# A group-normalised 3x3 convolution: statistics for 12 images at a time, measured further ahead

## The chip, the cores and the metric

The kernel runs on one core of a Trainium2 chip. The metric is the device time of one execution in microseconds (us), lower being better. The kernel before has a median of 968.84 us over three runs (968.79 to 969.57). The engines are named as in the profile: PE is TensorE (matrix products), PEld its weight loads, DVE is VectorE, ACT is ScalarE, POOL is GpSimd, and SP is SyncE, which here only issues DMAs.

## The reference

The input is 160 images of 128 channels and 32x32 pixels (float32). Each is normalised over groups of four channels, a 3x3 convolution with quantised weights is applied, and the image itself is added back:

```
def _gn(v, G=32, eps=1e-5):
    ...
    m = jnp.mean(g, axis=(2, 3, 4), keepdims=True)
    s = jnp.var(g, axis=(2, 3, 4), keepdims=True)
    return ((g - m) / jnp.sqrt(s + eps)).reshape(v.shape)
...
xb = x.reshape(B // N, N * C, H, W)
act = jax.lax.conv_general_dilated(xb, w, window_strides=(STRIDE, STRIDE), padding=[(PAD, PAD), (PAD, PAD)], dimension_numbers=('NCHW', 'OIHW', 'NCHW'), feature_group_count=N)
...
x = x + _L0_conv_ref(_gn(x), L0_conv_U)
```

There are five weight sets; image b*5 + n is convolved with set n. The weights are U rounded down in two steps that depend on the largest and smallest value of U. Here it matters only that every set costs some vector and scalar work, done while the images of the set before are convolved.

## The kernel before, in words

**Order of the images.** One loop (`for i in range(self.imgs)`, L1106) runs over 160 images, 32 of each weight set in turn. Each engine executes its instructions in the order in which this loop emits them. There are no planned times: what an engine waits for is decided by data and by buffers.

**An image in the pipeline.** Iteration i works on several images at once:

- ScalarE measures one image some way ahead, in two passes over its 1024 pixels. The first sums them (L241, stage 0), the second sums the squares of the differences (L248, stage 1). In the loop, stage 0 stands at the head of ScalarE's part of the iteration, ahead of `residual(i-1)`; stage 1 stands at its tail. Eight images, `BY_VECTOR = (8, 10, 11, 14, 19, 24, 29, 34)`, are measured by VectorE instead.
- For image i+4, POOL and VectorE take the mean off and combine neighbouring columns into a tile v of 2048 values ("combined" images: POOL L675 and L705 in `beside_pairs`, VectorE L687 and L694 in `combine`), or POOL normalises it into z (L711, the other images). POOL's part is tied to the last but one of VectorE's instructions ahead of `pairs`, so that it runs while VectorE is in `pairs`.
- For image i+3, ScalarE makes the float16 high part (L735 from v, or L645 from z). If the image is the first of its statistics group and not combined, ScalarE also makes z itself first (`normalise`, L637), from the group's `shift` and `rstd`.
- For image i+2, VectorE makes the float16 low part (L741, or L748 and the three operations L761 to L770).
- For image i+1, PE forms the products of rows (`sums_of_pairs`, into the PSUM tiles m1a or m1b, and m2, which is "m" in the profile). ScalarE copies m2 out (`leave`, L888), and VectorE writes both into the image's PSUM bank (`pairs`, L900 and L902).
- For image i, PE adds the rest of the products (`main`), and in the next iteration ScalarE copies the bank to SBUF (`residual`, L926). POOL issues a DMA that adds it to the output (L950). The image itself was stored to the output earlier by SP (`store_input`, L965).

The tile m2 is a single PSUM bank, so `leave` for image i+1 has to be done before PE starts the row products of image i+2.

**Statistics by group.** `cuts` (L472) divides the images into groups: small ones first, then 8 images each from image 24 on, 24 groups in all. `self.groups` and `group_of` follow from it. When the last image of a group has been measured, the group's numbers are made in the three iterations after:

- first: `means` (PE, L256), then on VectorE `deviations_by_vector` (five operations on 128x8 numbers, L296 to L302),
- second: `variances` (PE, L273), and `deviation` on ScalarE (L279),
- third: `power` on POOL (L286, which stands on POOL ahead of `beside_pairs` of image i+4), and after VectorE's `pairs` the two operations of `scales_by_vector` (L307: rstd times a constant; L309: shift = mean times rstd).

How far ahead is measured is set by one line, in which the lead grows by one for every fourth image up to a cap:

```
ahead = i + min(10 + i // 4, self.STAT_LEAD + 1)
to_measure = range(measured, min(self.imgs, ahead))
```

With STAT_LEAD = 14 the cap is reached at iteration 20. In the iterations 8, 12, 16 and 20 there are two images to measure in place of one.

**Loads and stores.** Images come in pairs ("chunks", 1 MB) into 12 buffers. Chunk c + 12 is loaded into the buffer of chunk c; `consumed(c)` says after which iteration that load is emitted, and the DMA itself waits until the buffer's last reader is done. Four iterations after its load is emitted, the chunk is stored to the output. Loads and stores go out on SP's queue, one after the other; the store of a chunk waits there until its load has landed.

Of the kernel before, what the change touches and what calls it, by code (L numbers as in the profile page):

```python
# [8 lines left out]
F32 = mybir.dt.float32  # L9
I32 = mybir.dt.int32  # L10
MM = mybir.dt.float16
ALU = mybir.AluOpType
# [9 lines left out]
NB = 2  # L22
# [14 lines left out]
class Later:  # L37


    def __init__(self, steps=(), pace=0.0):  # L40
        self.steps = iter(steps)
        self.pace, self.due = pace, 0.0
        self.scalar = False
# [19 lines left out]
    def finish(self):  # L63
        run(self.steps)
# [125 lines left out]
def group_mean_matrix(nc, pool):  # L190

    P = nc.NUM_PARTITIONS
    gavg = pool.tile([P, P // GROUP, GROUP], F32, tag="gavg", name="gavg")
    nc.gpsimd.memset(gavg, 1.0 / GROUP)
    nc.gpsimd.affine_select(
        out=gavg, in_=gavg, compare_op=ALU.is_ge, fill=0.0, base=0,
        pattern=[[-GROUP, P // GROUP], [0, GROUP]], channel_multiplier=1,
    )
    nc.gpsimd.affine_select(
        out=gavg, in_=gavg, compare_op=ALU.is_ge, fill=0.0, base=GROUP - 1,  # L200
        pattern=[[GROUP, P // GROUP], [0, GROUP]], channel_multiplier=-1,
    )
    return gavg.rearrange("p g k -> p (g k)")


class Statistics:
# [5 lines left out]
    def __init__(self, nc, small, gavg, mhalf, nb, scale, name):  # L212
        self.nc, self.small, self.gavg, self.mhalf = nc, small, gavg, mhalf
        self.nb, self.scale, self.name = nb, scale, name
        self.late = False

        self.mv = self.tile("mv", [nb, 2])

# [85 lines left out]
    def scales_by_vector(self):  # L304

        vector = self.nc.vector
        vector.tensor_scalar_mul(self.rstd, self.rstd, self.scale)  # L307
        self.shift = self.tile("shift", [self.nb])
        vector.tensor_tensor(self.shift, self.ngm, self.rstd, ALU.mult)  # L309

    def scales(self):
        nc = self.nc
# [8 lines left out]
def general_path(tc, keep, steps, x, u, out):  # L321
# [8 lines left out]
    with tc.If(far > 0), ExitStack() as ctx:  # L330
# [9 lines left out]
        for n in range(N_SETS):  # L340
            un = one.tile([P, C, TAPS], F32, tag="u", name=f"g_u{n}")
            nc.sync.dma_start(un, uv[n])
            wn = one.tile([P, C, TAPS], F32, tag="w", name=f"g_w{n}")
            k1, k2 = run(steps.quantise(one, un, f"g{n}", F32))
            nc.vector.tensor_scalar_mul(wn, k1, steps.s1)
            nc.vector.scalar_tensor_tensor(wn, k2, steps.s2, wn, ALU.mult, ALU.add)
# [38 lines left out]
class Main:  # L385
# [21 lines left out]

    STAT_LEAD = 14  # L410
    LOAD_LEAD = 18
    CHUNKS = 12
    STEADY = 7
# [3 lines left out]
    EARLY = 8  # L417
    FIRST = 3
    HURRIED = (0, 2, 4, 8, 24)


    COLS = (1, 0, 2)
# [3 lines left out]
    def __init__(self, tc, ctx, keep, x, u, out):  # L426
        self.tc = tc
        nc = self.nc = tc.nc
        self.imgs, C, self.H, self.W = x.shape
        P = self.P = nc.NUM_PARTITIONS  # L430
        assert C == P and self.H * self.W == 1024
        self.per_set = self.imgs // N_SETS
        self.xv = x.rearrange("(b n) c h w -> n c b (h w)", n=N_SETS)
        self.ov = out.rearrange("(b n) c h w -> n c b (h w)", n=N_SETS)
        self.uv = u.rearrange("n (o i k) -> n o i k", o=C, k=TAPS)

        def pool(name, bufs, **kw):
            return ctx.enter_context(tc.tile_pool(name=name, bufs=bufs, **kw))

        self.const = pool("const", 1)  # L440
        self.qpool = pool("quant", 1)
        self.wpool = pool("weights", 2)
        self.upool = pool("u", 1)
        self.xpool = pool("x", self.CHUNKS)
        self.zpool = pool("z", 2)
        self.parts = pool("parts", 4)
        self.rows = pool("rows", 4)
        self.wide = pool("wide", 2)
        self.wide_parts = pool("wide_parts", 3)
        self.evac = pool("evac", 2)  # L450
        self.sums = pool("sums", 3)
        self.unread = pool("unread", 1)
        self.small = pool("small", 3)
        self.ps_eo = pool("ps_eo", 2, space=PSUM)
        ps_m = pool("ps_m", 1, space=PSUM)
        ps_small = pool("ps_small", 1, space=PSUM)
        self.steps = Steps(nc, keep)

        self.m1a, self.m1b, self.m2_ps = (
            ps_m.tile([P, self.H // 2, self.W], F32, tag=name, name=name)  # L460
            for name in ("m1a", "m1b", "m2")
        )
        self.pair = [self.m1a, self.m2_ps]

        small = ps_small.tile([P, 512], F32, tag="small", name="small")
        self.pt, self.pg = small[:, : ROW * P].rearrange("p (k o) -> p k o", k=ROW), small[:, ROW * P :]
        self.chunks, self.z, self.hi, self.v, self.eo, self.m2 = {}, {}, {}, {}, {}, {}
        self.sum, self.stored = {}, {}
        self.tables, self.wts, self.across = {}, {}, {}
        self.columns = []  # L470

        cuts = [0, 2, 4, 8, 12, 16, 20, *range(24, self.imgs + 1, 8)]  # L472
        self.groups = [range(a, b) for a, b in zip(cuts, cuts[1:])]
        self.group_of = {i: k for k, g in enumerate(self.groups) for i in g}
        self.stats = {}
# [117 lines left out]
    def keep_sums(self, n, col):  # L593
        wt = self.wts[n, col]
        run(self.both_sums(
            self.nc.gpsimd, wt[:, self.SUM], wt[:, self.DIFF], *(wt[:, k] for k in range(ROW))
        ))
# [9 lines left out]
    def stats_of(self, k):  # L607
        if k not in self.stats:
            self.stats[k] = Statistics(
                self.nc, self.small, self.gavg, self.mhalf, len(self.groups[k]),  # L610
                self.steps.lift, k,
            )
            self.stats[k].late = self.groups[k].start not in self.HURRIED
        return self.stats[k]

    def measure(self, i, stages=(0, 1)):
# [39 lines left out]

    def by_scalar_too(self, i):

        return i < self.FIRST + 4 or i == self.groups[self.group_of[i]].start

    def column_of(self, i):

# [306 lines left out]

    def consumed(self, c):  # L970

        return max(i + 2 if self.by_hand(i) else i - 2 for i in range(c * NB, c * NB + NB))

    def run(self):
        nc, P = self.nc, self.P
# [26 lines left out]
        self.ident5 = self.const.tile([P, P], MM, tag="ident5", name="ident5")  # L1002
        nc.gpsimd.tensor_scalar_mul(self.ident5, ident, 5.0)
        self.gavg = group_mean_matrix(nc, self.const)
        self.mhalf = self.const.tile([P, 8], F32, tag="mhalf", name="mhalf")
        nc.gpsimd.memset(self.mhalf, -0.5)

        self.los = []
# [97 lines left out]
        for i in range(self.imgs):  # L1106
# [30 lines left out]
            else:  # L1137
                j = i - 1
                self.conv(i, on_the_way)
            ahead = i + min(10 + i // 4, self.STAT_LEAD + 1)  # L1140
            to_measure = range(measured, min(self.imgs, ahead))
# [163 lines left out]
```

## Time and profile before

| | before |
|---|---|
| median of three runs | 968.84 us |
| the profiled execution | 968.17 us |
| its span (first to last instruction) | 966.4 us |
| PE busy | 926.9 us (96%) |
| VectorE busy | 910.1 us (94%) |
| ScalarE busy | 862.0 us (89%) |
| POOL busy | 463.6 us (48%) |
| HBM traffic over the span | 262 GB/s |

The profile is of one execution. "Busy" is the time in which an engine had at least one instruction under way. PE's matrix products overlap: one of 512 columns is shown with 0.38 us, but the next starts about 0.21 us later. Idle time in front of an instruction is shown with what ended it ("<-"). The shares are averages over a start of some 50 us, a long middle part, and an end in which no image is left to measure.

### The profile page before, as it was taken

Reading aid. Unit: us, or ns where it says so; the run is one execution under the profiler, and the core shown is the slowest. Engines: PE = TensorE matmul, PEld = TensorE weight load, DVE = VectorE, ACT = ScalarE, POOL = GpSimd, SP = SyncE. Lnnn points to the kernel's source line nnn. Section 1 sums busy time; section 2 is a strip of 40 time slices with the busy share of each in tenths; the row PEclk is TensorE's granted clock in tenths of the full one; section 3 lists DMA queues with packets and bytes.
Section 4 is the critical chain, followed back from the end, with each engine's and each line's share of the span. In section 5 each row is a group of like instructions: output and inputs, shape, how many; then the busy total and the mean of one; then the engine's idle time right before and its main releaser. Section 6 shows DMA issues by size and latency. Waiting matters only on the chain.

```text
span 966.4 us, 13055 instructions
## 1 busy us (share of the span) xinstructions
PE 926.9 (96%) x4432; PEld 433.6 (45%) x4432; DVE 910.1 (94%) x1280; ACT 862.0 (89%) x1167; POOL 463.6 (48%) x477
## 2 busy tenths in 40 slices
PE   2999999999999999999999999999999999999997
PEld 1444444444444444444444444444444444444443
DVE  7999999999999999989999999999999998998995
ACT  5879999999999999999989999999989999998561
POOL 4345344446445444554355435534445545666550
PEclk9999999999999999999999999999999999999999
DMA  9079999999999999999999999999999999666663
GB/s 363 20 273 340 338 328 321 334 322 315 327 320 328 314 327 323 311 315 258 283 243 287 276 305 286 278 251 301 278 274 260 286 275 255 98 90 107 91 107 112
DMA packets 67450, 254.22 MB, mean 263 GB/s; under 512 B 5296, under 2 KB 5296, under 8 KB 67376
## 3 DMA queue, kind: packets, MB, share of 16 engines
q1 hardware_dynamic: 45344, 173.09, 47.6%
q0 software_dynamic: 22032, 80.23, 44.7%
q8 instruction: 36, 0.59, 0.2%
q14 instruction: 38, 0.31, 0.1%
HBM read 89.19 MB, written 164.10 MB: 262 GB/s over the span
## 4 chain that ended last, share of the span: by engine, by line


## 5 line engine op out<-in xcount | busy, mean ns | idle before, releaser
L785 PE MATMUL eo<-hi,wt 128*128 128x496 f16 (+3 forms) x1170 | 310.3, 375 | 0.9 <-ACT wt L567 0.9
L840 PEld LDWEIGHTS <-wt 128*128 128x128 f16 x1884 | 183.9, 99 | 211.5 <-DVE rows L770 1.7
L741 DVE SCALAR_TENSOR_TENSOR vl<-v,rstd,vh 128x2048 f16<-128x2048 f32 x94 | 221.5, 2356 | 1.0 <-ACT vh L735 0.9
L840 PE MATMUL eo<-vh,wt 128*128 128x512 f16 x561 | 210.2, 375 | 0.2 <-DVE eo L902 0.2
L840 PE MATMUL eo<-vl,wt 128*128 128x512 f16 x561 | 210.1, 375 | 0.0
L735 ACT ACTIVATE vh<-v,rstd 128x2048 f16<-128x2048 f32 x94 | 188.1, 2001 | 13.4 <-DVE v L694 13.0
L926 ACT COPY sum<-eo 128x1024 f32<-128x1024 f32 x153 | 160.7, 1050 | 29.4 <-PE eo L840 28.5
L675 POOL TENSOR_SCALAR v<-xt,ngm 128x64 f32<-128x64 f32 x94 | 83.0, 883 | 215.5 <-issue 66.8
L785 PEld LDWEIGHTS <-wt 128*128 128x128 f16 x1242 | 120.9, 99 | 140.2 <-DVE eo L902 2.6
L248 ACT ACTIVATE junk<-xt,mv 128x1024 uint8<-128x1024 f32 x152 | 174.4, 1147 | 0.1
L840 PEld LDWEIGHTS <-across 128*128 128x128 f16 x1128 | 110.3, 98 | 140.3 <-issue 13.3
L241 ACT ACTIVATE junk<-xt 128x1024 uint8<-128x1024 f32 x152 | 160.5, 1056 | 13.8 <-DMA xt<-in_x_dram 10.7
L711 POOL TENSOR_SCALAR z<-xt,ngm,rstd 128x1024 f32<-128x1024 f32 x49 | 90.5, 1847 | 155.9 <-DVE rows L769 45.9
L840 PE MATMUL eo<-rows,wt 128*128 128x512 f16 x378 | 143.5, 380 | 0.0
L950 POOL DMA_DIRECT2D out_dram<-sum x153 | 133.8, 876 | 9.5 <-ACT sum L926 6.1
L840 PE MATMUL m<-vl,across 128*128 128x496 f16 (+1 forms) x282 | 105.6, 374 | 9.5 <-DVE vl L741 9.5
L687 DVE TENSOR_TENSOR v<-xt 128x960 f32<-128x960 f32 x94 | 109.0, 1160 | 0.0
L840 PE MATMUL m<-vh,across 128*128 128x496 f16 (+1 forms) x282 | 105.6, 375 | 0.9 <-ACT m L888 0.9
L888 ACT ACTIVATE m<-m 128x512 f32<-128x512 f32 x157 | 93.8, 597 | 13.4 <-PE m L840 13.2
L705 POOL TENSOR_TENSOR v<-xt 128x512 f32<-128x512 f32 x94 | 97.2, 1034 | 0.0
L748 DVE TENSOR_TENSOR lo<-z,hi 128x1024 f16<-128x1024 f32 x66 | 80.6, 1220 | 0.0
L286 POOL TENSOR_TENSOR rstd<-ve,mhalf 128x8 f32<-128x8 f32 (+2 forms) x24 | 39.1, 1629 | 68.8 <-DVE rows L769 22.0
(150 smaller groups left out, 1182.3 us busy)
## 6 DMA issues: line engine op xcount, KB each, us to landing
xt<-in_x_dram SPq DMA_DIRECT2D x78, 1024.0 KB, 12.7
out_dram<-sum POOLq DMA_DIRECT2D x153, 512.0 KB, 8.8
out_dram<-xt SPq DMA_DIRECT2D x76, 1024.0 KB, 18.6
out_dram<-xt SPq DMA_DIRECT2D x7, 512.0 KB, 3.7
u<-in_L_conv_U_dram SPq DMA_DIRECT2D x4, 576.0 KB, 19.0
xt<-in_x_dram SPq DMA_DIRECT2D x4, 512.0 KB, 9.7
range<-in_L_conv_U_dram SPq DMA_DIRECT2D x3, 576.0 KB, 7.9
u<-in_L_conv_U_dram SPq DMA_DIRECT2D x2, 288.0 KB, 3.2
```

Of the source, the lines that this page charges most:

```text
L241: self.nc.scalar.activation(junk, image, ACTF.Copy, scale=-1.0 / image.shape[1], accum_out=self.mv[:, j, 0:1],)
L248: self.nc.scalar.activation(junk, image, ACTF.Square, bias=self.mv[:, j, 0:1], accum_out=self.mv[:, j, 1:2],)
L687: nc.vector.tensor_tensor(self.view(v, 1, (511, 2), (half, H), (1, half - 1)), self.view(x, 1, (1, 2), (W, H), (2, half - 1)), self.view(x ...
L705: ins = nc.gpsimd.tensor_sub(self.v[i][:, 1536:], odd, even)
L711: ins = nc.gpsimd.tensor_scalar(z, self.image(i), st.ngm[:, j], st.rstd[:, j], ALU.add, ALU.mult)
L735: self.nc.scalar.mul(vh, self.v[i], st.rstd[:, j])
L741: yield self.nc.vector.scalar_tensor_tensor(vl, self.v[i], st.rstd[:, j], self.hi[i], ALU.mult, ALU.subtract)
L785: nc.tensor.matmul(self.bank(target, a)[:, first:end, c0:c1], self.wts[n, col][:, k, :], tile[:, s0 : s0 + 2 * (end - first) - 1 : 2, c0 + ...
L840: self.nc.tensor.matmul(out, weights, moving, start=start and j == 0, stop=False, skip_group_check=True)
L888: self.nc.scalar.mul(m2, self.m2_ps, 0.5)
L926: nc.scalar.copy(self.as_banks(i, self.sum[i]), self.flat(i, eo))
L950: added = self.nc.gpsimd.dma_start(self.ov[n, :, b], self.sum.pop(i), accum_op=ALU.add)
```

## The change

The statistics groups have 8 images up to image 48, then 12 each up to image 144, then 8 again; there are 20 groups in place of 24. The cap of the lead is 20 images in place of 15 (STAT_LEAD 19), so it goes on growing until iteration 40: iterations 24, 28, 32, 36 and 40 now also measure two images. Groups that start at image 32 or later have no `shift` (L309 is left out), and their first image, where it isn't combined, gets its z from POOL like any other and not from ScalarE. The load of chunk c + 12 is emitted one iteration earlier. The constant -0.5 that `power` uses is 16 wide in place of 8.

```
-        self.late = False
+        self.late = self.shifted = False
...
         vector.tensor_scalar_mul(self.rstd, self.rstd, self.scale)
-        self.shift = self.tile("shift", [self.nb])
-        vector.tensor_tensor(self.shift, self.ngm, self.rstd, ALU.mult)
+        if self.shifted:
+            self.shift = self.tile("shift", [self.nb])
+            vector.tensor_tensor(self.shift, self.ngm, self.rstd, ALU.mult)
...
-    STAT_LEAD = 14
+    STAT_LEAD = 19
...
+    BY_SCALAR = 32
...
-        cuts = [0, 2, 4, 8, 12, 16, 20, *range(24, self.imgs + 1, 8)]
+        cuts = [0, 2, 4, 8, 12, 16, 20, 24, 32, 40, *range(48, self.imgs - 12, 12), 152, self.imgs]
...
             self.stats[k].late = self.groups[k].start not in self.HURRIED
+            self.stats[k].shifted = self.groups[k].start < self.BY_SCALAR
...
     def by_scalar_too(self, i):
-        return i < self.FIRST + 4 or i == self.groups[self.group_of[i]].start
+        start = self.groups[self.group_of[i]].start
+        return i < self.FIRST + 4 or i == start and start < self.BY_SCALAR
...
     def consumed(self, c):
-        return max(i + 2 if self.by_hand(i) else i - 2 for i in range(c * NB, c * NB + NB))
+        return max(i + 2 if self.by_hand(i) else i - 3 for i in range(c * NB, c * NB + NB))
...
-        self.mhalf = self.const.tile([P, 8], F32, tag="mhalf", name="mhalf")
+        self.mhalf = self.const.tile([P, 16], F32, tag="mhalf", name="mhalf")
```

## The prediction

> **What bounds the kernel now.** I read the page first, then stretches of the span, then the waits of PE and of ScalarE, and last the timelines where those waits end. The page says PE is busy nearly all the time; the stretches (busy us of each engine, number of instructions in brackets) say more:
>
> ```profile
> core 0: us, PE busy (x) PEld busy (x) DVE busy (x) ACT busy (x) POOL busy (x), PEclk, DMA share, GB/s
> 190.00:291.00 101.00, 101.00 (x485) 47.26 (x483) 97.79 (x136) 96.89 (x132) 49.48 (x49) 1.00 1.04 322
> 291.00:400.00 109.00, 109.00 (x530) 51.51 (x528) 105.62 (x150) 106.42 (x149) 50.26 (x51) 1.00 1.04 321
> 400.00:600.00 200.00, 197.20 (x945) 92.12 (x944) 191.11 (x263) 190.53 (x259) 96.99 (x93) 1.00 1.02 284
> 600.00:800.00 200.00, 198.06 (x951) 92.41 (x950) 193.71 (x266) 190.49 (x260) 96.13 (x95) 1.00 1.00 274
> 800.00:945.00 145.00, 142.10 (x677) 66.18 (x675) 132.75 (x154) 118.04 (x141) 83.51 (x73) 1.00 0.69 122
> ```
>
> The first stretch holds iterations 24 to 40. PE is busy in all of it, so time lost there is lost for good; VectorE and ScalarE are idle for 3.2 and 4.1 us of 101. Three engines stand near their limit at once, and the DMA engines show a share of 1. Only in the last stretch does ScalarE have room. What PE waits for after the start (us in total, times, longest):
>
> ```profile
> PE m L840 <- DVE vl L741: 9.5, 9, 1.9
> PE m L840 <- ACT m L888: 0.9, 1, 0.9
> PE m L840 <- DVE rows L770: 0.8, 1, 0.8
> ```
>
> So about 11 us are lost to engines that come late, nearly all to VectorE's low part. The timeline shows what makes it late (VectorE, then POOL, then PE; start, duration, idle time before):
>
> ```profile
> 810.25 0.70 DVE L902 SCALAR_TENSOR_TENSOR eo<-m1b,m 128x512 f32<-128x512 f32 x1
> 811.17 0.37 DVE L307 TENSOR_SCALAR rstd<-rstd,lift 128x8 f32<-128x8 f32 x1 [0.22 <-POOL rstd L286]
> 811.58 0.96 DVE L309 TENSOR_TENSOR shift<-ngm,rstd 128x8 f32<-128x8 f32 x1
> 812.46 1.15 DVE L687 TENSOR_TENSOR v<-xt 128x960 f32<-128x960 f32 x1
> ...
> 809.43 1.71 POOL L286 TENSOR_TENSOR rstd<-ve,mhalf 128x8 f32<-128x8 f32 x1 [5.91 <-DVE rows L769]
> 811.14 0.37 POOL L675 TENSOR_SCALAR v<-xt,ngm 128x64 f32<-128x64 f32 x1
> 811.48 1.03 POOL L705 TENSOR_TENSOR v<-xt 128x512 f32<-128x512 f32 x1
> ...
> 816.59 0.38 PE L840 MATMUL m<-vl,across 128*128 128x512 f16 x1 [0.97 <-DVE vl L741]
> ```
>
> This is a group's third step. `power` pushes POOL's two operations 1.7 us back; L309, on 8 numbers, lasts 0.96 us until POOL's L705 ends, and L687 starts only then, 1.5 us after `pairs` ends at 810.95. PE pays 0.97 us.
>
> ScalarE's own cost of one measured image, in iteration 25:
>
> ```profile
> 198.43 1.16 ACT L248 ACTIVATE junk<-xt,mv 128x1024 uint8<-128x1024 f32 x1
> 199.49 0.20 ACT L248 ACTIVATION_READ_ACCUMULATOR junk<-xt,mv 128x1 f32 x1
> 199.71 1.06 ACT L241 ACTIVATE junk<-xt 128x1024 uint8<-128x1024 f32 x1
> 200.68 0.19 ACT L241 ACTIVATION_READ_ACCUMULATOR junk<-xt 128x1 f32 x1
> 200.77 1.08 ACT L926 COPY sum<-eo 128x1024 f32<-128x1024 f32 x1
> ```
>
> From 198.43 to 200.77 is 2.34 us, with nothing between.
>
> **What the Trainium skill says.** "SBUF — State Buffer", section "SBUF: two separate sides": VectorE and GpSimd share a port pair under an exclusive lock; a VectorE operation with two SBUF inputs and a GpSimd operation that reads SBUF exclude each other, and whoever starts first holds it to the end. The trace agrees: L309 takes 0.16 us alone and 0.96 us beside L705. So leaving L309 out does not make L687 earlier, since L687 has two SBUF inputs too. "Perfetto Trace Analysis", section "Identifying the Most-Contended Engine": occupancy is a fair measure for Vector and Scalar, a poor one for Tensor. So I looked at the starts: products shown with 0.375 us start every 0.21 us in the PE lines of the timeline, whose overlap could hide a gap of up to 0.16 us; between 190 and 291 us the largest spacing of two starts is 0.23, so nothing is hidden. Section "Optimizing Scalar/DVE Operations" of the same page: each operation has a fixed overhead. The five operations on 128x8 numbers take 0.15 to 0.17 us each, so at 128x12 I take them as unchanged.
>
> **The change part by part**, against the profiled execution's 968.17 us (span 966.4 and 1.77 around it).
>
> *The growing lead.* Images 39, 44, 49, 54 and 59 become second images of iterations 24, 28, 32, 36 and 40. The earlier second images (19, 24, 29, 34) are VectorE's by the list BY_VECTOR, which the change leaves alone; the new ones fall to ScalarE. That is 5 x 2.34 = 11.7 us more in a stretch where ScalarE is idle for 101 - 96.89 = 4.1 us (2.7 waiting for PE at L926, 0.8 at L888). Queued behind the second stage 0 are `residual` and `leave`, and behind the second stage 1 those of the next iteration; `pairs` and PE's next row products wait for them. How late may they be? In the timeline the m copy ends at least about 1.2 us before PE overwrites that bank, in the tightest of five images (226.12 against 227.3 for image 31), and VectorE's start of `pairs` lies 0 to 2.9 us after it. So a backlog of some 1.2 us can be carried over at the end. PE loses 11.7 - 4.1 - 1.3 = **+6.3 us**. Bounds: 4.5 if two images' worth of lag can be carried, 9 if ScalarE's gaps can't be filled because VectorE falls behind with it. The five images that ScalarE is spared at the end (iterations 141 to 145) are worth 0: PE there waits for VectorE only.
>
> *Fewer groups.* From image 48 on there are 10 groups in place of 14. On PE each costs two insertions: products start at 805.14 and 805.50 around one pair of L273, so 0.36 - 0.22 = 0.14 us, twice per group, 4 groups: **-1.1 us**. VectorE saves 4 x 5 x 0.16 = 3.2 us, which counts only through PE's waits, next.
>
> *Third steps.* Of the 9.5 us, 7.65 us precede images 64, 74, 79, 119, 135, 143 and 151, a few images behind such a step. `power` takes 788 ns on 128x2 and 1763 on 128x8, so 0.16 us per number; on 128x12 an estimated 2.4 us. POOL's L675 and L705 and VectorE's L307 and L687 move back by another 0.65 us. From image 32 on there were 16 third steps, 11 beside a combined image; after there are 12, 10 beside a combined one (image p+4 for p = 28, 31, 43, 55, 91, 103, 115, 127, 135, 143). In two (p = 67, 79) POOL also has z, 1.2 to 3.2 us. Fewer steps, each longer. Taking each step's extra lateness against the time the low part had to spare at the next combined image (0.1 us at 59, 0.6 at 49, 1.7 at 94, nothing at 119), I get some 8.2 us lost in place of 7.6: **+0.6 us**. Bounds -7.65 (none is left) and +4.
>
> *No `shift`.* 0.16 us of VectorE where it ran alone, nothing beside L705: 0 on the path, being covered by that lock. Without the cover it would give back up to 0.96 us per step, which is inside the bounds above.
>
> *z by POOL.* ScalarE loses five L637 (images 48, 56, 88, 96, 128), 1.15 us each after overlap: 5.8 us. In their stretch (291 to 400) PE never waits, so 0; it only clears the carried backlog sooner. POOL gains five L711 of about 1.5 us, within its idle half: 0, up to +1.
>
> *Loads.* By order on SP's queue, the loads of chunks 16 to 23 go ahead of one more store each, and from chunk 24 on the order is the same. A store behind them lands some 5 us later, and the POOL DMA that adds image 12 may wait for it for 3 us of POOL's idle time: 0, bounds -1 and +2. Measuring up to five images earlier takes some 29 us off the time between landing and first use. The tightest is the load of images 54 and 55 (SP's queue; the store waits until it has landed):
>
> ```profile
> 226.92 5.42 SPq L495 DMA_DIRECT2D xt<-in_x_dram  x1
> ...
> 257.83 0.38 SPq L965 DMA_DIRECT2D out_dram<-xt  x1
> ```
>
> It lands at 257.8; the changed kernel wants it in iteration 36, which without any delay would begin at 256. Three second images have put ScalarE some 4 us back by then, so 0, bounds 0 and +5. The wider constant is set once, before the loop: 0.
>
> **Sum:** +6.3 - 1.1 + 0.6 = +5.8, so 974.0 us for a profiled execution; the median of runs lies 0.7 above the profiled one, hence **974.6 us**.
>
> **The rivals.** *The backlog is absorbed:* ScalarE's extra passes are taken up by waits and buffers, at 0 to 2 us. The total is 967.8 to 970.3, say 969, no measurable change. Against it: 4.1 us of idle time can't hold 11.7.
>
> *Loads come late:* ScalarE, in order, stands before images 50 to 63 until they land, DMA share being 1.04 there. Every late microsecond adds; some 4 us more give 978.6. For it: the landing margins above vanish. Against it: the delay of the first theory makes room.
>
> *Faster, by the third steps:* placed at other images of the five-image pattern, they no longer meet a low part without time to spare, and the 7.65 us go. With ScalarE's loss between its low end and its middle (4.5 to 6.3) this gives 968.84 - 1.1 - 7.65 + 5.4 = 965.5. It decides once ScalarE's loss is under 6.8 us with all those waits gone, or under 3 with half gone. For it: the same step costs 1.9 us at images 79 and 119 and nothing at others. Against it: each is 0.65 us longer.
>
> **How the numbers follow.** Runs here tell a difference of about 0.2% from none (966.9 to 970.8). Chances: forecast 0.52 (its own range 971 to 978), absorbed 0.10, loads late 0.17, faster 0.21. So faster 0.21, same 0.09, slower 0.70. The range that leaves out about 2 in 10 is 965.5 to 980.
>
> **What would show it.** Right: between 190 and some 300 us ScalarE has no idle time, PE shows gaps before L840 that end with ACT m or DVE vl, and 6 us are lost by iteration 41; `power` on 128x12 at 2.4 us; 8 products fewer each of L256 and L273. Wrong: PE still full from 190 to 300, or ScalarE's gaps ended by DMA, or the waits on vl down to 3 us.

## The result, and the profile after

The changed kernel is slower by 0.21%: 970.9 us against 968.67 us (medians of 20 runs each), a ratio of 1.0021 with a 95% interval of 1.0015 to 1.0028. The forecast was slower by 5.8 us; the loss is 2.2 us. The profiled execution took 971.39 us, its span is 969.6 us.

Three of the same stretches as before the change, of the changed kernel (busy us of PE, PEld, VectorE, ScalarE and POOL in this order):

```profile
190.00:291.00 101.00, 97.28 (x461) 44.55 (x459) 91.85 (x125) 100.27 (x143) 47.66 (x46) 1.00 1.04 328
291.00:400.00 109.00, 106.74 (x510) 49.37 (x509) 105.54 (x142) 103.76 (x143) 50.90 (x50) 1.00 1.03 300
...
800.00:945.00 145.00, 145.00 (x691) 67.59 (x690) 132.44 (x150) 111.96 (x128) 86.20 (x75) 1.00 0.72 131
```

Two things happened at once. In the first stretch, where PE had been full, ScalarE is now busy for 100.27 of 101 us and PE for 97.28; 24 fewer products start in it. In the last stretch PE had 2.9 us without work, and now has none. What PE waits for after the start:

```profile
PE m L844 <- DVE vl L745: 6.4, 8, 1.4
PE m L844 <- ACT m L892: 3.7, 5, 1.0
PE m L844 <- DVE rows L774: 1.6, 3, 0.8
PE eo L844 <- DVE eo L906: 1.2, 4, 0.4
```

Waits on VectorE's low part vl fell from 9.5 to 6.4 us, and waits on ScalarE's copy of m rose from 0.9 to 3.7. The place of the latter is iteration 24, the first with a new second image (timeline of ScalarE, then of PE):

```profile
190.53 1.06 ACT L241 ACTIVATE junk<-xt 128x1024 uint8<-128x1024 f32 x1
191.71 1.06 ACT L241 ACTIVATE junk<-xt 128x1024 uint8<-128x1024 f32 x1
...
196.11 1.15 ACT L248 ACTIVATE junk<-xt,mv 128x1024 uint8<-128x1024 f32 x1
...
197.38 1.15 ACT L248 ACTIVATE junk<-xt,mv 128x1024 uint8<-128x1024 f32 x1
...
200.61 0.60 ACT L892 ACTIVATE m<-m 128x512 f32<-128x512 f32 x1
...
201.26 0.38 PE L844 MATMUL m<-vh,across 128*128 128x512 f16 x1 [1.01 <-ACT m L892]
```

Both passes stand twice in a row, the copy of m ends at 201.21, and PE starts 0.05 us later after 1.01 us without work.

### The profile page after: what moved, and what is told of

Same layout as the page of the kernel before. It is cut to its first block, busy times and chain, and to the rows that moved or that the text cites. A ratio compares the mean times of both kernels' runs of the same rounds, so it can differ in the third digit from the quotient of the medians.

```text
span 969.6 us, 12968 instructions
## 1 busy us (share of the span) xinstructions
PE 928.7 (96%) x4416; PEld 431.4 (44%) x4416; DVE 903.9 (93%) x1240; ACT 857.0 (88%) x1158; POOL 468.7 (48%) x478
## 4 chain that ended last, share of the span: by engine, by line
## 5 line engine op out<-in xcount | busy, mean ns | idle before, releaser
L745 DVE SCALAR_TENSOR_TENSOR vl<-v,rstd,vh 128x2048 f16<-128x2048 f32 x94 | 220.4, 2344 | 0.8 <-ACT vh L739 0.6
L679 POOL TENSOR_SCALAR v<-xt,ngm 128x64 f32<-128x64 f32 x94 | 78.6, 836 | 236.2 <-issue 92.5
L715 POOL TENSOR_SCALAR z<-xt,ngm,rstd 128x1024 f32<-128x1024 f32 x54 | 96.2, 1782 | 161.1 <-DVE rows L773 46.9
L691 DVE TENSOR_TENSOR v<-xt 128x960 f32<-128x960 f32 x94 | 113.3, 1205 | 0.0
L709 POOL TENSOR_TENSOR v<-xt 128x512 f32<-128x512 f32 x94 | 96.9, 1031 | 0.0
L904 DVE SCALAR_TENSOR_TENSOR eo<-m1a,m 128x512 f32<-128x512 f32 x78 | 54.2, 695 | 22.5 <-PE m1a L844 11.6
## 6 DMA issues: line engine op xcount, KB each, us to landing
xt<-in_x_dram SPq DMA_DIRECT2D x78, 1024.0 KB, 10.6
```

Of the source, the lines that this page charges most:

```text
L691: nc.vector.tensor_tensor(self.view(v, 1, (511, 2), (half, H), (1, half - 1)), self.view(x, 1, (1, 2), (W, H), (2, half - 1)), self.view(x ...
L709: ins = nc.gpsimd.tensor_sub(self.v[i][:, 1536:], odd, even)
L715: ins = nc.gpsimd.tensor_scalar(z, self.image(i), st.ngm[:, j], st.rstd[:, j], ALU.add, ALU.mult)
L745: yield self.nc.vector.scalar_tensor_tensor(vl, self.v[i], st.rstd[:, j], self.hi[i], ALU.mult, ALU.subtract)
```

## The experiments

Theory 1 is that of the prediction: the second images of iterations 24, 28, 32, 36 and 40 give ScalarE more than it can do in that stretch. Theory 2 was formed on the trace after the change, for what the prediction had not foreseen, the end without waits: whether a third step costs PE time depends on where it falls, since that decides when `power` may start. All ratios are to the kernel before. The name in brackets is that of the run.

**The five second images left out** (`five_left_out`).

```
+        if i in (39, 44, 49, 54, 59):
+            if 1 in stages:
+                self.nc.scalar.copy(st.mv[:, j, :], st.mv[:, j - 1, :])
+            return
```

> The changed kernel without ScalarE's two passes over images 39, 44, 49, 54 and 59; their two numbers per channel are copied from the neighbouring image in one small ScalarE operation, so the statistics of these five images are left out. Theory 1 (the second images of five iterations overload ScalarE): the gaps that PE shows between 190 and 325 us in the changed kernel, some 6.6 us, go, and the time falls from 970.9 to 964.3 (963.3 to 965.3). Rival (the gaps come from the longer statistics steps or from z made by POOL, not from the passes): 970 to 971.

Measured 964.74 us, ratio 0.9955 (0.9938 to 0.9971). Against the changed kernel's 1.0021 this is 0.0066, or 6.4 us. The interval leaves some 1.6 us either way. PE is busy again for 100.82 of the 101 us from 190 on. Theory 1 stands: the passes cost about 6.4 us, and without them the changed kernel would be the faster one. This kernel keeps the earlier loads and POOL's z, so neither is what held PE up in that stretch.

**The passes given to VectorE** (`five_by_vector`).

```
-    BY_VECTOR = (8, 10, 11, 14, 19, 24, 29, 34)
+    BY_VECTOR = (8, 10, 11, 14, 19, 24, 29, 34, 39, 44, 49, 54, 59)
```

> The changed kernel with images 39, 44, 49, 54 and 59 measured by VectorE, like the earlier second images. VectorE takes about 1.75 us per image (two L231, one L233, L234 and L235 by the kernel before), 8.7 us in all, and was idle for 3.2 us of 101 between 190 and 291 us. Theory 1 in its wide form (both engines are full there, so the passes cost PE time wherever they go): 969.5 (968.5 to 971). Rival (only ScalarE was short of time): 964.5 to 966.

Measured 970.21 us, ratio 1.0018 (1.0009 to 1.0026), not to be told from the changed kernel. The stretch from 190 to 291, and what PE waits for:

```profile
190.00:291.00 101.00, 97.52 (x465) 45.14 (x464) 99.36 (x148) 93.37 (x127) 47.43 (x46) 1.00 1.04 328
...
PE m L844 <- DVE vl L745: 8.4, 10, 1.8
PE m L844 <- DVE rows L774: 2.8, 4, 1.4
PE m L844 <- ACT m L892: 0.9, 1, 0.9
```

ScalarE now has 7.6 us to spare and VectorE 1.6; PE is as short of work as in the changed kernel (97.52 us busy there against 97.28), only the name of what it waits for is another. Both engines are nearly full there, and the extra work cost PE time on either.

**The lead alone** (`lead_alone`).

```
-    STAT_LEAD = 14
+    STAT_LEAD = 19
...
-        return max(i + 2 if self.by_hand(i) else i - 2 for i in range(c * NB, c * NB + NB))
+        return max(i + 2 if self.by_hand(i) else i - 3 for i in range(c * NB, c * NB + NB))
```

> The kernel before with the cap of the lead at 20 images and the loads emitted one iteration earlier, nothing else: groups of 8, shift and ScalarE's z kept. Theory 1: ScalarE's five extra passes cost 6.6 us between 190 and 325 us. Theory 2 (a statistics step costs PE time only where the image two ahead of it isn't combined, since power may then start only after VectorE's last short operation): the steps now fall in iterations 127, 135 and 143, with a combined image two ahead, and the three waits of about 1.1 us of the end go. Together 968.7 + 6.6 - 3.4 = 971.9 (970.5 to 973). Rival (the extra passes are absorbed): 966 or less.

Measured 971.01 us, ratio 1.0021 (1.0012 to 1.0031): the whole loss of the change. By the spacing of PE's starts the waits of 1 us at the end are gone (two of under 0.1 us are left), with shift and with groups of 8. So the end can be freed without larger groups and without leaving shift out; what is left is where the steps now fall, which `phase_zero` below tries.

**Groups of 8 with the long lead** (`eight_at_19`), the changed kernel with the old cuts:

```
-        cuts = [0, 2, 4, 8, 12, 16, 20, 24, 32, 40, *range(48, self.imgs - 12, 12), 152, self.imgs]
+        cuts = [0, 2, 4, 8, 12, 16, 20, *range(24, self.imgs + 1, 8)]
```

> The changed kernel with groups of 8 throughout, all else kept: the lead grows to 20, no shift and POOL's z from image 32 on. It differs from lead_alone (971.0) by shift and z only, and from the changed kernel (970.9) by the size of the groups only. Leaving shift out was worth some 1.1 us in shift_kept, so 970 (969 to 971), and groups of 12 are worth nothing, what they save in products being lost to longer steps. Rival (groups of 12 carry a gain that the lead hides): 972 or more.

Measured 970.36 us, ratio 1.0012 (1.0005 to 1.0019). No gain of the larger groups shows: by the ratios groups of 8 are 0.9 us faster, and the intervals overlap. Larger groups save products on PE, but PE's waits after the start are 12.9 us with them and 10.5 with groups of 8. `power` took 2.34 to 2.72 us on 128x12 in seven of the eight groups (4.13 in the eighth), against 1.66 to 1.96 on 128x8 before the change.

**Shift kept** (`shift_kept`).

```
-            self.stats[k].shifted = self.groups[k].start < self.BY_SCALAR
+            self.stats[k].shifted = True
```

> The changed kernel with shift computed for every group again, and not used from image 32 on. Reading of the prediction (the operation lies under POOL's lock of the shared port, so leaving it out moves nothing): 970.9, within 0.7 either way, and L687's successor takes its 1.15 us again with 0.96 us for shift ahead of it. Rival (the missing shift is what freed the end): waits on vl come back behind the steps of iterations 135 and 143, and 972 or more.

Measured 972.4 us, ratio 1.0038 (1.0024 to 1.0052). The end stays free (waits of under 0.1 us), so the rival falls; but the time is above the changed kernel, by 1.6 us going by the ratios and by 1.2 going by each kernel's median against the kernel before, where 0 was expected. The intervals overlap, so the size is uncertain. Where POOL's L709 (before: L705) runs, leaving shift out does nothing, as predicted; here is a step of the changed kernel:

```profile
653.87 1.99 DVE L691 TENSOR_TENSOR v<-xt 128x960 f32<-128x960 f32 x1
```

The operation behind L307 is now L691 (before: L687), and it takes 1.99 us in place of 1.15: what shift waited is now part of it. In the trace of `shift_kept`, shift takes 0.97 us beside L709 in the steps of iterations 55, 91, 103, 115 and 127, and PE's waits on vl behind 55 and 115 are the same with and without it. In the steps of 34, 43, 67, 79, 135 and 143 it takes 0.17 us, and behind three of these PE waits longer: from 0.63 to 0.84 us after 43, from 0.08 to 0.33 after 67, and from 0.80 to 1.02 after 79. That is 0.7 us of the 1.2 to 1.6; where the rest lies is open.

**A lead of 16 with groups of 8** (`lead15_eight`), the changed kernel with the old cuts and one more edit:

```
-    STAT_LEAD = 19
+    STAT_LEAD = 15
```

> The changed kernel with groups of 8 throughout and the cap at 16 images, so only image 39 is measured as a second one and the statistics steps come one iteration earlier than before. Theory 1: about 1.2 us lost to ScalarE near 200 us. Theory 2: no wait on vl behind the steps of iterations 131, 139 and 147, 3.4 us less than before; in all 966 to 967. Rival (the waits at the end went because groups are larger): those waits stay, 969 to 970.

Measured 962.84 us, ratio 0.9943 (0.9927 to 0.996), lower than expected and faster than both kernels. Only one of the new second images is left, and one wait of 1.0 us behind it; in the end PE waits for nothing.

**The same with the last steps back in their old place** (`phase_zero`).

```
+        cuts = [0, 2, 4, 8, 12, 16, 20, *range(24, 129, 8), 133, 141, 149, 157, self.imgs]
```

> As lead15_eight (962.8), but the last groups are cut at 133, 141, 149 and 157, so that their third steps fall in iterations 128, 136 and 144, where the image two ahead isn't combined, as before the change; one more group. Theory 2: waits on vl of about 1 us come back behind two or three of these steps, 965.3 (964 to 967). Rival (an earlier finish of the statistics is what helped, wherever the step falls): 962.8 to 963.5.

Measured 965.44 us, ratio 0.9966 (0.9955 to 0.9978), 2.6 us above lead15_eight. The one more group accounts for some 0.3 us of this, an estimate from the prediction's 0.14 us twice per group. From 800 us on, where lead15_eight has no wait, PE waits again, behind two of the three steps:

```profile
PE m L844 <- DVE vl L745: 1.7, 2, 0.9
```

At the end of the kernel the place decides. Why it does is seen in the changed kernel's step of iteration 135 (POOL, then VectorE, below the first line), to be laid beside the one of iteration 132 in the prediction. The first line belongs to the latter: it is what released `power` there.

```profile
808.86 0.42 DVE L769 TENSOR_TENSOR rows<-lo 128x512 f16<-128x512 f16 x1
...
829.85 3.29 POOL L286 TENSOR_TENSOR rstd<-ve,mhalf 128x8 f32<-128x8 f32 x1
...
833.49 1.03 POOL L709 TENSOR_TENSOR v<-xt 128x512 f32<-128x512 f32 x1
...
829.27 2.34 DVE L745 SCALAR_TENSOR_TENSOR vl<-v,rstd,vh 128x2048 f16<-128x2048 f32 x1
...
833.67 0.70 DVE L906 SCALAR_TENSOR_TENSOR eo<-m1a,m 128x512 f32<-128x512 f32 x1
...
834.47 1.15 DVE L691 TENSOR_TENSOR v<-xt 128x960 f32<-128x960 f32 x1
```

`power` is tied to the last but one VectorE instruction ahead of `pairs`. In iteration 132 that is L769, which ends 0.25 us before `pairs` begins at 809.53. In iteration 135 image 137 is combined, the last instruction is the long L745, and the one before it ends ahead of that. So `power` starts when POOL is free, beside L745. It is through, even at 3.29 us, before `pairs` ends at 834.37, and L691 starts on time.

**`power` untied** (`before_power_free`), in the kernel before:

```
-                        self.after(st.power(), before)
+                        st.power()
```

> The kernel before with power no longer tied to VectorE's last but one instruction: POOL may start it as soon as ScalarE has made its input and POOL is free, in the iteration before. Theory 2 (a late start of power pushes POOL's two operations for the next combined image, and these hold L687 back): the waits on vl behind the steps of iterations 132, 140, 148 and 76, 116 shrink, 968.7 - 5 = 964 (962.5 to 966). Rival (VectorE pays in any case, as power then shuts it out of operations with two SBUF inputs elsewhere): 968 to 971.

Measured 961.97 us, ratio 0.9927 (0.991 to 0.9943): this one line makes the kernel before 7.1 us faster, a little more than the range expected. Waits on vl after the start fall from 9.5 to 3.1 us. The step that cost PE 0.97 us in the prediction's timeline, now (POOL, then VectorE):

```profile
803.28 2.01 POOL L286 TENSOR_TENSOR rstd<-ve,mhalf 128x8 f32<-128x8 f32 x1 [2.43 <-ACT ve L279]
...
806.78 0.42 POOL L675 TENSOR_SCALAR v<-xt,ngm 128x64 f32<-128x64 f32 x1 [1.49 <-issue]
...
804.33 1.22 DVE L748 TENSOR_TENSOR lo<-z,hi 128x1024 f16<-128x1024 f32 x1
...
808.54 1.16 DVE L687 TENSOR_TENSOR v<-xt 128x960 f32<-128x960 f32 x1
```

`power` is done 1.5 us ahead of POOL's next work, and L687 starts 0.25 us after `pairs` ends (808.29) in place of 1.5. VectorE's L748 takes the usual 1.22 us beside it, so the rival falls too.

**`power` untied in the changed kernel** (`after_power_free`), the same edit.

> The changed kernel with power no longer tied to VectorE's last but one instruction. Theory 2: its waits on vl and rows behind the third steps after 325 us (6.1 us) mostly go, while the 6.6 us of ScalarE's backlog between 190 and 325 us stay: 966 (965 to 967). Rival (with 12 numbers power is too long to fit anywhere without shutting VectorE out): 969 or more.

Measured 964.24 us, ratio 0.9955 (0.9938 to 0.9971), better than expected. Waits on vl fall from 6.4 to 2.0 us; those on m stay (3.7, now 4.4). So removing the one loss leaves the other.

**The second image at a better place** (`lead15_at28`), lead15_eight with the lead growing in iteration 28:

```
-            ahead = i + min(10 + i // 4, self.STAT_LEAD + 1)
+            ahead = i + min(10 + i // 4, self.STAT_LEAD + (i >= 28))
...
-    BY_SCALAR = 32
+    BY_SCALAR = 40
```

> As lead15_eight (962.8), but the lead grows from 15 to 16 images in iteration 28 in place of 24, so image 43 is the second one; shift is left out from image 40 on. In the kernel before, ScalarE has just come out of a backlog at iteration 24 and waits 1.2 us for PE at iteration 28. Theory 1: the one wait of PE on ScalarE's m copy near 200 us (1.17 us) goes or shrinks, 961.8 (961 to 962.7). Rival (ScalarE has no room at any place): 962.8 or more.

Measured 962.36 us, ratio 0.993 (0.9914 to 0.9947). By the time it can't be told from lead15_eight (962.84). In the profile the wait on m near 200 us is gone, and waits on vl are 0.6 us more (3.9 against 3.3).

**Both together** (`lead15_at28_power_free`): that kernel with `power` untied.

> lead15_at28 (962.4) with power untied as in before_power_free (962.0). Theory 2: of its waits after 325 us (2.9 us) some 1 to 2 us go, 960.8 (959.8 to 961.8). Rival (the two remove the same waits): 962 or more.

Measured 959.24 us, ratio 0.9898 (0.9882 to 0.9915), the fastest of all and again a little below the range expected: 1.0% below the kernel before, with 4.4 us of PE's waits left after the start.

**What the waits leave out.** PE's idle time leaves out what the overlap of its products hides, up to 0.16 us at each wait. An estimate from the spacing of PE's starts (what goes beyond 0.215 us, from 60 us on to 25 us before the end, the small statistics products left out) gives a loss of 13.8 us before, 17.3 in the changed kernel, 8.3 in lead15_eight, 10.6 in phase_zero, 6.8 and 10.7 with `power` untied in the kernel before and in the changed one. With the prediction's 0.14 us twice per group for their number, the differences between these fit the measured ratios within 0.5 us. Three runs fit less well: the estimate gives 4.9 of the 6.4 us of five_left_out, 5.6 of the 6.8 of lead15_at28 and 8.2 of the 9.9 of the fastest kernel. What the rest is stays open.

## Why the prediction was right or wrong

- *The growing lead, +6.3 us:* right in place and mechanism, and in size as far as it is known. Leaving the five images out gave 6.4 us, 1.6 either way; ScalarE's idle time went, and PE's gaps end with ScalarE's m or VectorE's late parts. The rivals that the backlog is absorbed and that loads come late fall: ScalarE waited for no load between 190 and 330 us.
- *Third steps, +0.6 us:* this is the step that failed. PE's waits on vl after 330 us, before and after the change:

```profile
PE m L840 <- DVE vl L741: 7.6, 7, 1.9
...
PE m L844 <- DVE vl L745: 4.1, 5, 1.1
```

With 0.2 us each on rows and on the bank, the waits on VectorE fell from 7.6 to 4.5 us, so the term is -3.1. I let every step push POOL's two operations back by the length of `power`, and asked only how much time the low part had to spare. But how far they are pushed depends on when `power` may start, and that on which VectorE instruction stands last ahead of `pairs`. The five steps with the longest waits before the change (iterations 76, 116, 132, 140, 148) all have an image two ahead that isn't combined; after it, the three of the end have a combined one, and cost nothing where I had them cost more. A combined image two ahead is no guarantee: the steps of iterations 55 and 115 still cost about 1 us each, and in these `power` was released by L142, an operation of the next set's weights that stands behind L745. Nor does one that isn't combined always cost: PE waits 1.1 us in all behind the step of 79, but not behind those of 36, 44, 84 and 124 before the change and of 91 after it; which of them had time to spare, and why, was not worked out. I also had two of the twelve steps in the wrong place: those of the groups that start at images 32 and 40 fall in iterations 27 and 34, not 28 and 31, and neither stands beside a combined image. With the five images left out, PE shows no wait on VectorE behind either, so this did not make the difference.
- *`power` on 128x12, 2.4 us:* nearly right, 2.6 where it ran undisturbed by L745.
- *Fewer groups, -1.1 us:* the products are fewer as said (36 of L256 after the start in place of 44); what that saves was not measured alone. With -3.1 and +6.4 it gives the measured +2.2; that the fit is so close is luck, as the 6.4 is known only to 1.6 us. By eight_at_19 it is paid back by the longer steps.
- *No shift, 0:* beside L705 or L709 leaving it out moves nothing, as argued. Where it ran alone, its 0.16 us were put at nothing although a low part without time to spare can follow: shift_kept points to a gain of 1.2 to 1.6 us, and its trace shows 0.7 of it behind three such steps. Two of these stand after 330 us, so 0.5 us of it lie within the -3.1.
- *z by POOL, loads, the wider constant, 0:* nothing in the traces speaks against it; they were not tried one by one. Of the five L637, only those of images 48 and 56 lie between 291 and 400 us as I had it; the others start at 540, 585 and 769 us. After 330 us PE waits for ScalarE in neither trace, so the 0 stands.

The rival that the third steps get cheaper was half right: it needed all of their waits gone, or ScalarE's loss under 3 us with half gone.

## What to carry to other kernels

An average hides when work falls due: five passes of 2.34 us were free by the page (ScalarE 89% busy) and cost about 6.4 us where they fell, within some 100 us in which three engines were nearly full. And when an operation is moved or lengthened, ask first what releases it: a tie that was made to keep two engines apart held a 1.7 us operation back until it lay on the path, and taking it off gained 7.1 us of 969.

## What the runs showed of the hardware that was not expected

`power` on 8 numbers did not keep VectorE out of the shared port while it ran. Beside it, in the step with `power` untied shown above, VectorE's L748, with two SBUF inputs, took its usual 1.22 us, although it started 1.1 us into `power` and ended 0.3 us after it. Here the measurement goes against the rule from which the prediction argued, that whoever starts first holds the port to the end. The other way round `power` was held up: started at 829.85 beside L745, it ended 1.5 us after that had finished (831.61), having taken 3.29 us in place of 1.7. It was the same 1.5 us after L687 in other steps of the kernel with `power` untied. POOL's L705 (L709 after the change), which reads 512 numbers of each of two operands, held up L309 and L691 to its end (0.96 us in place of 0.16, and 1.99 in place of 1.15). Why `power` and L705 differ in this was not tried.
